# Gathers issued two at a time in the first graph layer and in the attention, and a node's own product moved to the end of the second graph layer

## The chip, the cores and the metric

The kernel runs on one core of one Trainium2 chip. The metric is the device time in microseconds. The engines are called as the profile calls them: PE (TensorE), PEld (its weight loads), DVE (VectorE), ACT (ScalarE), POOL (GpSimd) and SP (SyncE, which here only issues DMAs).

## What is computed

Four layers work on 6250 nodes of 256 values in fp32, each on the layer norm of the nodes, each added to them:

```
x += gnn0(norm(x))    # h = relu([x[src], edge_attr] @ W1 + b1) over 106250 edges sorted by dst;
                      # mean of h over each node's edges; relu([x, mean] @ W2 + b2)
x += moe0(norm(x))    # graph attention over 131072 random edges and own loops gives 16 values
                      # a node, a gate of the top 2 of 4 experts; the experts are 256-512-256, gelu
x += gnn1(norm(x))    # below
x += moe1(norm(x))    # shared network and top 2 of 4 small experts
```

The third one is where a product moves:

```
h   = relu(x @ Wp.T + bp)                       # 128 values a node
agg = segment_sum(edge_vals * h[src]**2, dst)
return h @ W1.T + b1 + sqrt(agg) @ W2.T + b2
```

`h @ W1.T` is the node's own product. It depends on no edge.

## The kernel before

Nodes lie in 49 tiles of 128 (T = 49). `x_all` and `b_all` keep 49 x 256 values a partition in SBUF for the whole kernel: `x_all` the running sum, `b_all` what the present layer needs of each node. The program is fully unrolled. The tile framework puts in the semaphores and may move an instruction on its engine's queue ahead of others that wait; otherwise the order is that of the code. Three tables lie in DRAM and are gathered from: `y_dram` (x @ W1 for the first layer, 256 values a node), `gat_dram` (24 values) and `hp_dram` (128 values). A `gather` (L1103) is one indirect DMA on POOL's queue: 128 rows, one to a partition. DMAs other than gathers go on SP's queue, a few on ACT's.

**Start** (L1310 to L1359): the nodes are loaded and normed, `y_dram` is written, edge windows are made.

**Stage 1, first graph layer** (L1362 to L1546). For each tile of 128 nodes a window of 18 x 128 edges is taken in three groups of six (`groups1`, G1 = 6). A group's edge values come on SP (`load_attr`), its six source rows by six gathers into one tile `yg` of [P, 6, D], three of them in turn (`load_sources`, L1382). Work goes by pairs of 128 edges (`pairs`, NPC = 3 a group): `turn` transposes a pair on PE, with ACT copying it out; `hidden` multiplies (four products of 256 columns), adds the gathered rows on DVE (L1417) and takes the Relu on ACT into `hbuf` (L1422); once a group `add_up` sums over nodes with 0/1 matrices (L1443). The loop L1523 runs `turn` three pairs ahead and `hidden` one pair ahead. At the second pair of a group (L1534) `load_sources` is called for two groups on; its tile is free when the group before is through `hidden`. For the groups 1 to 3 a copy of one column of `hbuf` into `seen` on POOL (L1386) holds the gathers until a named activation is done. `end_of` finishes a tile of nodes in pieces between the pairs. A generator, `background`, sorts the attention's edges on DVE.

**Stage 2, attention and experts** (L1554 to L2153). The attention's sorted edges come in 80 groups of 8 x 128 (NA = 80, G = 8). The loop L2113 does one group a turn, in a pipeline five deep: `fetch(k)` at the head of the turn issues eight gathers into the tile `sg` (five in turn), `score` works on group k - 2, `weigh` on k - 3, `spread_out` on k - 4 and `add_up` on k - 5. `weigh` and the first half of `spread_out` (L1743) read the gathered rows; the latter frees the tile. Between these stand six calls of `slot`, written out by hand. A `slot` advances the experts by one piece (`experts1`: `first` makes products and gelu, L1607, into `hh`, two in turn; `second` the second product, with its sums stored to DRAM) and every waiting step of `node_values` by one.

`node_values` (L1949) ends the layer for two tiles of nodes and begins the next one: it adds the experts' outputs with their gates to `x_all` (L1956), norms (L1976), adds the row b1 + b2 of the second graph layer to `x_all` (L1980), transposes (L1987), copies out to `b_all` (L1988), multiplies by Wp (L1992), takes the Relu into a small tile `ht` (L1994), transposes that into one half of a PSUM tile `py` (L1998), multiplies `ht` by `w1t` into the other half (L1999), squares the first half (L2001), adds the second half to `x_all` (L2002) and stores the square to `hp_dram` (L2003). The pool of `py` has two buffers, which the experts' second product uses too.

**Stage 3, second graph layer's edges and the last network** (L2160 to L2469). 139 groups of six chunks of 128 edges: `fetch` gathers four groups ahead (six buffers, L2382), `weights_of` makes weighted 0/1 matrices on DVE (L2390), `add_up` sums on PE (L2411). When a block of nodes has all its edges, `roots` takes the square root (L2423) and `end_of2` multiplies by W2 (`w2t`, L2228), adds to `x_all` (L2229), norms, transposes into `b_all` and makes the gate's logits. Then `gates2` and `experts2` work on the block, in pieces between the groups. There are 10 blocks of four tiles, three of two and three of one.

Of the kernel before, what the change touches and what calls it, by code (L numbers as in the profile page):

```python
# [8 lines left out]
F32 = mybir.dt.float32  # L9
# [832 lines left out]
def kernel(ctx: ExitStack, tc: tile.TileContext, a: dict, out: bass.AP):  # L842
# [74 lines left out]
    with ExitStack() as fast:  # L917
# [362 lines left out]
        with ExitStack() as layer:  # L1280
# [81 lines left out]
            with (  # L1362
# [8 lines left out]
                hbuf = [wy.tile([P, G1, WS], F32, name=f"h{i}") for i in range(2)]  # L1371
                seen = wy.tile([P, 1], F32, name="seen")
                sources, equals, et, sums = {}, {}, {}, {}
# [7 lines left out]

                def load_sources(q):  # L1382

                    if 1 <= q <= 3:
                        p, j = (q - 2, G1 - 1) if q > 1 else (0, 0)
                        GP.tensor_copy(seen, hbuf[p % 2][:, j, 0:1])  # L1386
                    w, g = groups1[q]
                    sources[q] = wk.tile([P, G1, D], F32, name="yg", bufs=3)
                    for j, (k, t) in enumerate(chunk(g)):
                        gather(sources[q][:, j, :], y_dram, src1[:, w, k, t : t + 1])  # L1390

# [15 lines left out]
                def hidden(k):  # L1407
                    q, j = pairs[k]
                    ph = psh.tile([P, 2, D], F32, name="ph")
                    e = et.pop(k)  # L1410
                    for i in range(2):
                        mm(
                            ph[:, i, :], lambda c: e[:, i, c * P : (c + 1) * P],
                            lambda c: w1b[:, c, :],
                        )
                    y = sources[q][:, j : j + 2, :]
# [5 lines left out]
                    SC.activation(h[:, j : j + 2, 0:D], y, AF.Relu)  # L1422
# [94 lines left out]
                work = [background()]  # L1517
                load_sources(0)
                for k in range(3):
                    turn(k)  # L1520
                hidden(0)
                load_sources(1)
                for k in range(len(pairs)):  # L1523
                    if k + 3 < len(pairs):
                        turn(k + 3)
                    if k + 1 < len(pairs):
                        hidden(k + 1)

                    q = k // NPC
                    if k % NPC == 0 and q:  # L1530
                        add_up(q - 1)
                    if k == len(pairs) - 1:
                        add_up(q)
                    if k % NPC == 1 and q + 2 < len(groups1):  # L1534
                        load_sources(q + 2)
                    for n in list(work):
                        if next(n, work) is work:
                            work.remove(n)
                    if k % (NPC * NG) == 0 and k:
                        work.append(end_of(k // (NPC * NG) - 1))  # L1540
                    if k == len(pairs) - 1:
                        work.append(end_of(T - 1))
# [28 lines left out]
        def experts1():  # L1571
# [24 lines left out]
            def first(u, f0):  # L1596
# [9 lines left out]
                for f in (f0, f0 + 1):  # L1606
                    SC.activation(  # L1607
                        hidden[u][:, f, :n, :], ph[:, f - f0, :n, :], AF.Gelu,
                        bias=b1[:, e, f : f + 1],
                    )  # L1610

            def second(u, i):
# [37 lines left out]
        def advance(queue, n):  # L1650
            for _ in range(n):
                if queue and next(queue[0], queue) is queue:
                    queue.pop(0)

        layers = [experts1()]
        part = sums.tile([P, 3, T, H], BF16, name="part")
        with (
# [32 lines left out]

            def fetch(g):
                got[g] = wk.tile([P, G, GW], F32, name="sg", bufs=5)
                for j in range(G):
                    gather(got[g][:, j, :], gat_dram, src2[:, g * G + j : g * G + j + 1])
# [234 lines left out]
            with nc.allow_non_contiguous_dma(reason="a bias, one element a partition"):  # L1929
                SY.dma_start(bp, a["L1_gnn_bp"].rearrange("(c p) -> p c", p=P))  # L1930
            w1t = w6.tile([P, D], F32, name="w1t")
            SY.dma_start(w1t, a["L1_gnn_W1_T"])
            b1 = bcast_row(w6, "b1", a["L1_gnn_b1"])
            V.tensor_add(b1, b1, bcast_row(n6, "xn", a["L1_gnn_b2"]))
            ys = {}
# [13 lines left out]
            def node_values(ws):  # L1949
# [22 lines left out]
                )  # L1972
                xns, hts = {}, {}
                for i, w in enumerate(ws):
# [4 lines left out]
                    )  # L1979
                    V.tensor_add(x_all[:, w, :], x_all[:, w, :], b1)  # L1980
                    yield False
# [8 lines left out]
                for w in ws:  # L1990
                    ph = psy.tile([P, 2, D], F32, name="py")[:, 0, 0:P]
                    mm(ph, lambda c: wpt[:, c, :], lambda c: b_all[:, w, c * P : (c + 1) * P])  # L1992
                    hts[w] = n6.tile([P, P], F32, name="ht")
                    SC.activation(hts[w], ph, AF.Relu, bias=bp)  # L1994
                    yield False
                for w in ws:
                    py = psy.tile([P, 2, D], F32, name="py")
                    TE.transpose(py[:, 0, 0:P], hts[w], ident)  # L1998
                    mm(py[:, 1, :], lambda c: hts[w], lambda c: w1t, 1)  # L1999
                    hp = n6.tile([P, PD], F32, name="hp")  # L2000
                    SC.activation(hp, py[:, 0, 0:P], AF.Square)  # L2001
                    V.tensor_add(x_all[:, w, :], x_all[:, w, :], py[:, 1, :])  # L2002
                    SY.dma_start(nodes(hp_dram)[:, w, :], hp)  # L2003
                    yield False
# [108 lines left out]
            for k in range(NA + 5):  # L2113
                if k < NA:
                    fetch(k)
                if k == 1:
                    own_edges()
                now, here, there, before = k - 2, k - 3, k - 4, k - 5
                if 0 <= before < NA:
                    add_up(before, 0)  # L2120
                slot()
                if now in range(NA):
                    score(now, 0)
                slot()
                if here in range(NA):
                    weigh(here)
# [3 lines left out]
                run(routing, False)  # L2130
                slot()
                if 0 <= before < NA:
                    add_up(before, 1)
                slot()
                if now in range(NA):
                    score(now, 1)
# [27 lines left out]
        with (  # L2164
# [8 lines left out]
            w2t = wp.tile([P, D], F32, name="w2t")  # L2173
            SY.dma_start(w2t, a["L1_gnn_W2_T"])
            gw = load_rows(wp, "gw", a["L1_ffn_gW"])
            gb = bcast_row(wp, "gb", a["L1_ffn_gb"])
# [46 lines left out]
            def end_of2(b, i, root):  # L2223
# [3 lines left out]
                pm = psm.tile([P, D], F32, name="pt")  # L2227
                mm(pm, lambda c: root[:, i, :], lambda c: w2t, 1)  # L2228
                V.tensor_add(x_all[:, w, :], x_all[:, w, :], pm)  # L2229
# [189 lines left out]
            def roots(b):  # L2419
                n = blocks[b][1]  # L2420
                root = wk.tile([P, BT, P], F32, name="gt")[:, 0:n, :]
                pe = sums.pop(b)[:, 0 : n * P].rearrange("p (w k) -> p w k", k=P)
# [118 lines left out]
```

## Time and profile before

| | |
|---|---|
| median of the runs, us | 3580.82 (3578.01 to 3580.89, three runs) |
| the profiled execution's own time, us | 4368.05 |
| its span, first to last instruction, us | 4366.3 |
| mean granted PE clock in it | 0.866 |
| instructions | 57680 |
| gathers in stages 1, 2, 3 | 882, 640, 831 |
| first and last gather start, us | 131.5 and 1674.3; 1713.7 and 2984.1; 3074.0 and 4286.1 |
| moved by DMA, mean | 428.52 MB, 98 GB/s |

The profile is of one execution, whose own time is longer than that of the runs without a profile. In a line of a group the columns are: code line, engine, operation, tile written <- tiles read, count; then the busy time in us and the mean of one in ns; then how long the engine had been idle before such instructions, with what ended most of that idle time. "issue" is idle time in which the engine waited for nothing that the profile shows; "remote" is a release that it cannot place. A product of fp32 operands stands in the trace as two records, each with its weight load.

### The profile page before, as it was taken

To read this page: it belongs to the slowest core of one execution; us is meant where nothing else is said; L and a number is where in the kernel's file an instruction comes from. 1 tells how busy PE (TensorE), PEld (TensorE's weight loads), DVE (VectorE), ACT (ScalarE), POOL (GpSimd) and SP (SyncE) were. 2 spreads that over 40 slices of the span, in tenths; PEclk is the share of its full clock that TensorE was granted. 3 is DMA by queue.
4 is the path that set the end of the run, shared out by engine and by line. 5 is a ranking of instruction groups with operands and counts; after the bars stand their busy time and mean duration, and the time that the engine had idled before them with its cause. 6 is when DMAs were issued, how large, how long until landed. Compare 5 with 4: busy or idle time off the path is not lost.

```text
span 4366.3 us, 57680 instructions
## 1 busy us (share of the span) xinstructions
PE 3529.8 (81%) x20063; PEld 2739.8 (63%) x20063; DVE 2183.1 (50%) x6292; ACT 1397.3 (32%) x2752; POOL 2243.2 (51%) x2367
## 2 busy tenths in 40 slices
PE   8788899998989987787888889888435776767888
PEld 3566666666666766576777777677334554544666
DVE  9788774333433333565646464656222343333445
ACT  4333333333333333232443433445001111211223
POOL 0455555555555554445444444442566666666651
PEclk9899999999999999899999999989557676776778
DMA  5445545555445443222424232333211121111210
GB/s 155 125 149 157 138 155 160 153 150 157 146 147 160 146 145 99 68 72 63 110 69 112 63 107 67 93 85 89 61 47 46 51 57 50 50 51 49 55 47 25
DMA packets 342929, 428.52 MB, mean 98 GB/s; under 512 B 139174, under 2 KB 246453, under 8 KB 342630
## 3 DMA queue, kind: packets, MB, share of 16 engines
q1 hardware_dynamic: 245174, 244.98, 18.7%
q0 software_dynamic: 89408, 178.08, 16.1%
q8 instruction: 162, 2.65, 0.2%
q10 hardware_dynamic: 8048, 1.68, 0.2%
q14 instruction: 137, 1.12, 0.1%
HBM read 382.05 MB, written 42.49 MB: 97 GB/s over the span
## 4 chain that ended last, share of the span: by engine, by line
PE 61%; another core or an unknown queue 11%; issue 11%; DVE 10%; ACT 4%; DMA 1%; POOL 1%; SPq 0%; DVEq 0%; ACTq 0%
PE ph L1091 26%; PE py L1091 10%; PE pt L1085 7%; PE pe L2411 5%; PE pe L1443 5%; PE po L1771 3%; PE pt L1091 3%; DVE key L1240 1%; PE pa L1708 1%; DMA rb<-low_dram 1%; DVE order L1237 1%; DVE eq L2390 1%; DVE pp L1750 1%; ACT L1607 1%
## 5 line engine op out<-in xcount | busy, mean ns | idle before, releaser
L1104 POOL DMA_INDIRECT yg<-y_dram,src x882 | 841.7, 954 | 822.8 <-ACT h L1422 338.7
L1104 POOL DMA_INDIRECT hg<-hp_dram,src x831 | 784.4, 944 | 446.3 <-issue 227.5
L1104 POOL DMA_INDIRECT sg<-gat_dram,src x640 | 611.6, 956 | 663.7 <-DVE px L1743 333.3
L1091 PE MATMUL ph<-w1b,et 128*128 128x256 f32 x3528 | 887.9, 394 | 28.0 <-issue 25.3
L1091 PEld LDWEIGHTS ph<-w1b,et 128*128 128x128 f32 x3528 | 662.9, 198 | 122.7 <-issue 45.6
L1417 DVE TENSOR_TENSOR yg<-ph,yg 128x512 f32<-128x512 f32 x441 | 299.8, 686 | 496.4 <-PE ph L1091 172.9
L2411 PEld LDWEIGHTS pe<-eq,hg 128*128 128x128 f32 x2036 | 377.7, 264 | 210.7 <-issue 143.5
L2411 PE MATMUL pe<-eq,hg 128*128 128x96 f32 (+15 forms) x2036 | 386.9, 344 | 146.4 <-issue 87.0
L1091 PE MATMUL py<-w,hh 128*128 128x256 f32 x1568 | 414.0, 402 | 61.3 <-ACT hh L1607 40.3
L2390 DVE TENSOR_SCALAR eq<-px,dst,ew 128x96 f32<-128x96 f32 x831 | 261.0, 367 | 320.4 <-remote 129.9
L1091 PE MATMUL ph<-b_all,w 128*128 128x256 f32 (+1 forms) x1600 | 410.7, 397 | 4.8 <-issue 4.7
L1086 ACT ACTIVATE et<-pt 128x512 f32<-128x512 f32 x441 | 259.5, 594 | 411.5 <-PE pt L1085 222.1
L1091 PEld LDWEIGHTS py<-w,hh 128*128 128x128 f32 x1568 | 298.7, 199 | 115.3 <-ACT hh L1607 47.8
L1422 ACT ACTIVATE h<-yg 128x512 f32<-128x512 f32 x441 | 275.6, 629 | 229.3 <-DVE yg L1417 180.7
L1091 PEld LDWEIGHTS ph<-b_all,w 128*128 128x128 f32 x1600 | 306.9, 201 | 45.7 <-issue 8.1
L1085 PE MATMUL pt<-ident,ea 128*128 128x128 f32 x1764 | 288.8, 285 | 33.6 <-issue 18.0
L1443 PE MATMUL pe<-h,eq 128*32 128x257 f32 x3168 | 254.1, 387 | 62.6 <-issue 35.2
L1085 PEld LDWEIGHTS pt<-ident,ea 128*128 128x128 f32 x1764 | 218.1, 148 | 110.5 <-issue 69.9
L1771 PE MATMUL po<-pp,B 128*128 128x240 f32 (+10 forms) x1280 | 269.2, 350 | 21.8 <-issue 12.1
L1607 ACT ACTIVATE hh<-ph,b 128x256 f32<-128x256 f32 (+1 forms) x400 | 165.7, 467 | 367.2 <-remote 130.4
L1771 PEld LDWEIGHTS po<-pp,B 128*128 128x128 f32 x1280 | 227.0, 198 | 38.9 <-issue 13.9
L1443 PEld LDWEIGHTS pe<-h,eq 128*32 128x32 f32 x3168 | 104.5, 109 | 190.4 <-issue 92.7
(331 smaller groups left out, 4328.3 us busy)
## 6 DMA issues: line engine op xcount, KB each, us to landing
ea<-in_edge_attr_dram SPq DMA_DIRECT2D x147, 768.0 KB
y<-y SPq DMA_DIRECT2D x196, 128.0 KB
w<-in_L_ffn_W_dram SPq DMA_DIRECT2D x48, 512.0 KB
y<-ys SPq DMA_DIRECT2D x96, 256.0 KB
rb<-low_dram SPq DMA_DIRECT2D x80, 256.0 KB
yg<-y_dram,src POOLq DMA_INDIRECT x882
hg<-hp_dram,src POOLq DMA_INDIRECT x831
sg<-gat_dram,src POOLq DMA_INDIRECT x640
```

The lines of the kernel that those rows point to most:

```text
L1085: TE.transpose(pt[:, c, :], src[:, c * P : (c + 1) * P], ident)
L1086: SC.activation(dst, pt.rearrange("p c k -> p (c k)"), AF.Copy)
L1091: TE.matmul(dst, lhs(c), rhs(c), start=c == 0, stop=c == n - 1)
L1104: GP.indirect_dma_start(out=dst, out_offset=None, in_=table[0:NP, :], in_offset=IndirectOffsetOnAxis(ap=idx, axis=0),)
L1237: V.max(out=top, in_=key)
L1417: V.tensor_add(y, ph, y)
L1422: SC.activation(h[:, j : j + 2, 0:D], y, AF.Relu)
L1443: TE.matmul(sums[w][b * Q : (b + 1) * Q, :], eq[k][:, j, at], h[:, i * NT + j, :], start=g == 0 and j == NT - 1, stop=g == last_of[b] and ...
L1607: SC.activation(hidden[u][:, f, :n, :], ph[:, f - f0, :n, :], AF.Gelu, bias=b1[:, e, f : f + 1],)
L1771: TE.matmul(po.rearrange("p b v -> p (b v)"), B[:, j, :], pp[:, j, 0:n, :].rearrange("p b v -> p (b v)"), start=half == 0 and j == 0, stop ...
L2390: V.tensor_scalar(equals[k][:, j, :], lanes[:, 0:NW], dst_of[:, t : t + 1], ew[:, t : t + 1], op0=OP.is_equal, op1=OP.mult,)
L2411: TE.matmul(sums[b][:, lo - t0 * P : hi - t0 * P], hg[:, j, :], eq[:, j, lo - n0 : hi - n0], start=False, stop=after >= (t0 + n) * P,)
```

## The change

In the **first layer**, `load_sources` takes a pair rather than a group. Its tile is [P, 2, D], nine in turn, so the memory is the same. For the pairs 3 to 8 a copy on POOL writes the first column of the new tile from an activation in `hbuf`, and the gathers follow into the same tile. The loop calls it up to twice a pair until it is six pairs ahead, then once a pair. A tile is free when the pair three before the present one is through `hidden`.

In the **attention**, `fetch` takes two chunks rather than eight, and is called four times a turn, after the first, second, third and fourth `slot`. From the second group on, a copy on POOL ahead of each two gathers writes one column of their rows from the newest expert activation (`newest`, set at the end of `first`).

In the **second graph layer**, the Relu's result is written over the first half of the tile's row in `b_all`, where it stays. The product by `w1t`, its add to `x_all` and the add of the bias row leave `node_values`. In stage 3 `end_of2` makes both products into one PSUM tile, `roots` adds the bias row to a whole block, and `w1t` and the two bias rows are loaded at the stage's head.

```diff
-                def load_sources(q):
-
-                    if 1 <= q <= 3:
-                        p, j = (q - 2, G1 - 1) if q > 1 else (0, 0)
-                        GP.tensor_copy(seen, hbuf[p % 2][:, j, 0:1])
+                def load_sources(k, after):
+
+                    q, j = pairs[k]
                     w, g = groups1[q]
-                    sources[q] = wk.tile([P, G1, D], F32, name="yg", bufs=3)
-                    for j, (k, t) in enumerate(chunk(g)):
-                        gather(sources[q][:, j, :], y_dram, src1[:, w, k, t : t + 1])
+                    sources[k] = wk.tile([P, 2, D], F32, name="yg", bufs=3 * NPC)
+
+                    if NPC <= k < 3 * NPC:
+                        p, i = pairs[after]
+                        h = hbuf[p % 2][:, i, 0:1]
+                        GP.tensor_copy(sources[k][:, :, 0:1], h.unsqueeze(1).to_broadcast([P, 2, 1]))
+                    for i, (n, t) in enumerate(list(chunk(g))[j : j + 2]):
+                        gather(sources[k][:, i, :], y_dram, src1[:, w, n, t : t + 1])
...
                     if k + 1 < len(pairs):
                         hidden(k + 1)
+                    for _ in range(2):
+                        if loaded < min(k + 2 * NPC + 1, len(pairs)):
+                            load_sources(loaded, k + 1)
+                            loaded += 1
...
-                    if k % NPC == 1 and q + 2 < len(groups1):
-                        load_sources(q + 2)
...
+                newest[0] = hidden[u][:, f0, 0, 0:1]
...
-            def fetch(g):
-                got[g] = wk.tile([P, G, GW], F32, name="sg", bufs=5)
-                for j in range(G):
+            def fetch(g, j0):
+
+                if j0 == 0:
+                    got[g] = wk.tile([P, G, GW], F32, name="sg", bufs=5)
+                if g > 0:
+                    GP.tensor_copy(
+                        got[g][:, j0 : j0 + 2, 0:1],
+                        newest[0].unsqueeze(1).to_broadcast([P, 2, 1]),
+                    )
+                for j in range(j0, j0 + 2):
                     gather(got[g][:, j, :], gat_dram, src2[:, g * G + j : g * G + j + 1])
...
-                    V.tensor_add(x_all[:, w, :], x_all[:, w, :], b1)
...
-                    hts[w] = n6.tile([P, P], F32, name="ht")
-                    SC.activation(hts[w], ph, AF.Relu, bias=bp)
+
+                    SC.activation(b_all[:, w, 0:P], ph, AF.Relu, bias=bp)
...
-                    TE.transpose(py[:, 0, 0:P], hts[w], ident)
-                    mm(py[:, 1, :], lambda c: hts[w], lambda c: w1t, 1)
+                    TE.transpose(py[:, 0, 0:P], b_all[:, w, 0:P], ident)
                     hp = n6.tile([P, PD], F32, name="hp")
                     SC.activation(hp, py[:, 0, 0:P], AF.Square)
-                    V.tensor_add(x_all[:, w, :], x_all[:, w, :], py[:, 1, :])
...
                 slot()
+                if k < NA:
+                    fetch(k, 0)
                 if now in range(NA):
                     score(now, 0)
                 slot()
+                if k < NA:
+                    fetch(k, 2)
...
                 slot()
+                if k < NA:
+                    fetch(k, 4)
...
                 slot()
+                if k < NA:
+                    fetch(k, 6)
...
-                mm(pm, lambda c: root[:, i, :], lambda c: w2t, 1)
+                mm(
+                    pm, lambda c: (b_all[:, w, 0:P], root[:, i, :])[c],
+                    lambda c: (w1t, w2t)[c],
+                )
...
             def roots(b):
                 n = blocks[b][1]
+                at = slice(blocks[b][0], blocks[b][0] + n)
+                V.tensor_add(
+                    x_all[:, at, :], x_all[:, at, :],
+                    b12[:, None, :].to_broadcast([P, n, D]),
+                )
```

More of the change, by code (lines that the diff above doesn't have):

```diff
@@ L1371 @@
                 hbuf = [wy.tile([P, G1, WS], F32, name=f"h{i}") for i in range(2)]
-                seen = wy.tile([P, 1], F32, name="seen")
                 sources, equals, et, sums = {}, {}, {}, {}
@@ L1415, in hidden @@
                         )
-                    y = sources[q][:, j : j + 2, :]
+                    y = sources.pop(k)
                     V.tensor_add(y, ph, y)
@@ L1517 @@
                 work = [background()]
-                load_sources(0)
+                for k in range(NPC):
+                    load_sources(k, None)
                 for k in range(3):
@@ L1521 @@
                 hidden(0)
-                load_sources(1)
+                loaded = NPC
                 for k in range(len(pairs)):
@@ L1653, in advance @@
                     queue.pop(0)
+        newest = [None]
         layers = [experts1()]
@@ L1930 @@
                 SY.dma_start(bp, a["L1_gnn_bp"].rearrange("(c p) -> p c", p=P))
[L1931 to L1934, printed above, removed]
             ys = {}
@@ L1972, in node_values @@
                 )
-                xns, hts = {}, {}
+                xns = {}
                 for i, w in enumerate(ws):
@@ L2113 @@
             for k in range(NA + 5):
-                if k < NA:
-                    fetch(k)
                 if k == 1:
@@ L2174 @@
             SY.dma_start(w2t, a["L1_gnn_W2_T"])
+            w1t = wp.tile([P, D], F32, name="w1t")
+            SY.dma_start(w1t, a["L1_gnn_W1_T"])
+            b12 = bcast_row(wp, "b12", a["L1_gnn_b1"])
+            V.tensor_add(b12, b12, bcast_row(wp, "b2", a["L1_gnn_b2"]))
             gw = load_rows(wp, "gw", a["L1_ffn_gW"])
```

## The prediction, made before the result was known

> **What bounds the kernel now.** I read the page's busy lines and slices first, then busy time by stage, then the waits of the lines that the change touches, and last the start times of single instructions. The page (engine, busy us, share of the span; below them the span in 40 slices, in tenths):
>
> ```profile
> PE 3529.8 (81%) x20063; PEld 2739.8 (63%) x20063; DVE 2183.1 (50%) x6292; ACT 1397.3 (32%) x2752; POOL 2243.2 (51%) x2367
> ...
> PE   8788899998989987787888889888435776767888
> ...
> POOL 0455555555555554445444444442566666666651
> PEclk9899999999999999899999999989557676776778
> ```
>
> The PE row changes at slice 28, and POOL is fuller after it. Busy time by stage (start, the first graph layer, attention with the experts, the second graph layer with the last network; columns are length, then busy us of each engine, granted clock, DMA share, GB/s):
>
> ```profile
> 0.00:130.00 130.00, 106.15 (x306) 51.18 (x306) 123.63 (x379) 61.88 (x160) 0.71 (x7) 0.97 0.47 140
> 130.00:1700.00 1570.00, 1399.98 (x9092) 1060.95 (x9093) 800.67 (x2124) 571.31 (x1225) 842.29 (x885) 0.95 0.51 149
> 1700.00:3074.00 1374.00, 1140.72 (x7141) 967.28 (x7140) 789.96 (x2013) 539.83 (x952) 615.77 (x644) 0.93 0.33 83
> 3074.00:4366.00 1292.00, 882.92 (x3526) 660.39 (x3526) 468.85 (x1779) 224.29 (x416) 784.42 (x831) 0.69 0.18 48
> ```
>
> In stages 1 and 2 TensorE is busy 89% and 83% at nearly full clock: they are TensorE's. In stage 3 it has 68% at a low clock. There the gathers set the pace. POOL's groups (busy, mean ns of one, idle before them), then two of its waits in stage 3 (us, times, longest):
>
> ```profile
> L1104 POOL DMA_INDIRECT yg<-y_dram,src x882 | 841.7, 954 | 822.8 <-ACT h L1422 338.7
> L1104 POOL DMA_INDIRECT hg<-hp_dram,src x831 | 784.4, 944 | 446.3 <-issue 227.5
> L1104 POOL DMA_INDIRECT sg<-gat_dram,src x640 | 611.6, 956 | 663.7 <-DVE px L1743 333.3
> ```
>
> ```profile
> POOL hg L1104 <- remote: 107.6, 35, 6.0
> ...
> POOL hg L1104 <- PE pe L2411: 65.4, 18, 7.9
> ```
>
> One gather is 0.945 us and 0.30 us of issue follow: 1.25 us from start to start. 831 of them are 1039 us of the 1212 between the first start (3074) and the last (4286); POOL waits 107.6 + 65.4 = 173 us, 14%, mostly for buffers that TensorE has not finished with.
>
> **The profiled execution and the median.** The profiled one took 4368 us (span 4366), the median is 3581: 787 us less. Floors from spacing say where these are not. A 256-column fp32 record is 0.216 us after the one before it in unbroken runs, a 128-column one 0.109. Stage 1: 3528 x 0.216 + 1764 x 0.109 + 3168 x 0.054 (four quarters side by side) + some 85 for the ends of nodes = 1210 us. Stage 2: 3168 x 0.216 = 684, po 217, pa and counting 56, node values 58 = 1015. Stage 3: POOL's 1039, and the 80 after the last gather. With the start's 130: 3474, an estimate. So unprofiled all stalls together are some 107 us, where the profiled execution has 892. Terms that are work at pace I carry over whole, terms that are stalls at about a third.
>
> **What the Trainium skill says.** "TensorE: Matmul & The Clock Gate", What's actually happening: the array's clock is halved until it has been busy. The trace agrees: the w2t records of stage 3 stand 0.426 us apart at the median against 0.218 for the w1t ones of stage 2. "Perfetto Trace Analysis", DMA Instruction — SWDGE (GPSIMD): the end shown is that of making descriptors, not of the data. The trace agrees: at the start of stage 3 the data land 2.40 us after the issue on the chain. "SBUF — State Buffer", Who interferes with whom: some VectorE instructions lock GpSimd out. Here it hardly shows: yg gathers have minimum 940, median 946 and maximum 2060 ns.
>
> **The change, part by part.**
>
> *Node's own product out of stage 2.* The groups, then three lines of who waited for L2002 (us, times):
>
> ```profile
> L1091 PE MATMUL py<-w1t,ht 128*128 128x256 f32 x98 | 30.7, 397 | 0.0
> L1980 DVE TENSOR_TENSOR x_all<-x_all,b 128x256 f32<-128x256 f32 x49 | 20.3, 418 | 7.7 <-ACT xn L1976 6.9 <-ACT b_all L1988 0.5
> L2002 DVE TENSOR_TENSOR x_all<-x_all,py 128x256 f32<-128x256 f32 x49 | 20.2, 414 | 16.5 <-ACT hp L2001 12.2 <-issue 4.2
> ```
>
> ```profile
>   PE py L1998: 21.5, 9
>   PEld py L1987: 20.7, 8
>   PE py L1987: 17.6, 7
> ```
>
> (a) TensorE loses 98 x 0.218 = 21 us of pace, in a stage that is its own: -21, whole. (b) The PSUM buffer py is freed by the square (L2001), not by VectorE's add (L2002). That is 0.45 to 5.7 us sooner, 1.38 on average over the 49 pairs in the trace. The PE matmul waits are 21.5 + 17.6 = 39 us (the weight loads' waits are the same time again); part would wait for the square or for something else: I take half, -20 profiled, -7 at the median; ends 0 and -39. (c) VectorE loses 40.5 us. It is busy 790 of 1374, so I count none; if it paced the stage, up to -40. (d) The Relu goes into b_all rather than ht: same instruction, 0. (e) In the tail of stage 2 (3030 to 3074) the last nodes are a chain of single instructions, with some four adds and two products off it: -3.
>
> *The same product in stage 3.* (f) 98 records more in end_of2; w2t, the nearest row, has 45.3 us busy for its 98 in this stage, 21 at full clock. The new product reads b_all and w1t, loaded long before, and stands next to w2t, so no wait is added. (g) VectorE: ten adds of 128x1024 at 1.22 us (nearest: 1.215 for L1783), three of 512 at 0.69, three of 256 at 0.42: 15.5 us, of 1292 with 469 busy. Behind them in VectorE's queue stand the equality tiles (L2390) that add_up needs. Both lie beside POOL's gathers while TensorE keeps within the six gather buffers. It fails to in 14% of the time, so 14% of 45.3 + 15.5 = 8.6 reaches POOL; I take +8 profiled, +6 at the median. Cover gone: +45 and more. (h) After the last gather some six nodes are still to end: +3. (i) Three loads move from SP's queue in stage 2 to the head of stage 3, at about 0.4 us each, where the last hp stores still pass: 0 to +1.2, taken as 0, as VectorE waits 2.9 us there for those stores anyway.
>
> *Gathers in twos, attention.* The same 640 gathers, plus 79 x 4 = 316 copies on POOL, each waiting for the newest expert activation. Nearest: the three `seen` copies, 183 to 197 ns; from copy to gather 0.35 us from start to start. 316 x 0.35 = 111 us more for POOL, which has 616 + 166 of issue in 1374: covered. Behind each copy only gathers are queued; weigh needs them three turns later, some 45 us. ScalarE writes the hh buffer anew two units on, some eight slots, so it should not wait for a copy: 0, bounds 0 to +10.
>
> *Gathers in twos, first layer.* As many gathers, three copies more (1 us on POOL, free). Pair 3's gathers now wait for pair 1's activation, not pair 0's: up to 3 us later while POOL fills the pipeline: +2. Steadily, POOL needs 2 x 1.25 = 2.5 us a pair against TensorE's 1210 / 441 = 2.7; waits for gather data are only 13.1 us in the whole tile's list.
>
> *Runs of gathers.* Adding up every start-to-start distance on TensorE beyond 0.45 us: in the first four gathers of an unbroken POOL run it lost 11 of 670 us (stage 1) and 23 of 376 (stage 2); from the fifth gather on 57 of 441 and 60 of 431. The run of 40 gathers at 1713 to 1764 has TensorE at one bf16 record in 1.4 to 2.1 us. Twos break such runs. But the cause may be the recording itself, since in the median all stalls are 107 us: I take -15 profiled, -5 at the median; ends 0 and -117.
>
> Sum, profiled: -21 - 20 - 3 + 8 + 3 + 2 - 15 = -46, 4368 to 4322. At the median: -21 - 7 - 3 + 6 + 3 + 2 - 5 = -25: **3556 us**.
>
> **Rivals.** *The runs are real* (0.18): half of the 107 us of stalls goes with them. Then -55 for -5: 3506. For it: the counts above. Against: stage 3 has the longest runs and no such budget. *Stage 3 takes it back* (0.16, slower): TensorE's add_up, not POOL, paces it wherever buffers are returned late. All 45.3 us of (f) then reach the end, with the 3 of (h): -34 + 48 = +14, 3595. It decides once TensorE's work for a group of six exceeds POOL's 7.5 us; for it, POOL's 173 us of waits and the 16.8% that add_up's products have on the chain from 3400 to 4200; against, the 25.9% that an unknown queue (the gathers' data) has there. *The change doesn't do what it says* (0.13): stage 2 is paced by the chain from scores through VectorE and ScalarE, and the freed TensorE time becomes a wait for DVE za or ACT hh (TensorE's second expert product waits 40.3 us for ACT hh as it is). Then (a) and (b) give -9 for -28 and the runs 0: 3581 - 9 - 3 + 11 = 3580.
>
> **How the numbers follow.** The forecast has 0.53, with 3537 to 3567 as its own range: (b) and (c) at their full ends, a third of 20 and of 40, make -19 or so more, the copies and (i) at theirs +11. The range runs from the first rival's time, with half of its cases beyond it, to just past the slower one: 3505 to 3600. About 0.2%, 7 us, is what a measurement can tell from no change. Faster by more: 0.53 + 0.18 = 0.71; within: 0.13; slower: 0.16.
>
> **What would show it.** Right: in stage 2 no L2002 in TensorE's waits, PE busy down by about 31, the stage 25 to 60 us shorter; in stage 3 the w-products at 196 records, POOL's gather spacing still 1.25 us, its waits up by under 15 us. Wrong: stage 3 longer by over 30 us; ScalarE's gelu waiting for a POOL copy; weigh waiting for gather data; or stages 2 as long as before with TensorE idler.

## The result, and the profile after

The changed kernel takes **3559.13 us** (median of five runs, 3557.47 to 3560.89), the kernel before, run beside it, 3578.01 (3574.05 to 3580.89). The ratio is 0.9947 (95% interval 0.9935 to 0.9958): 19 us or 0.5% less. The forecast was 3556.

One thing has to be known to read any number here: on three other chips these kernels take some 700 to 800 us longer, with 4368 to 4384 us for the kernel before (the **long level**, as against the **short level** of 3578 to 3581); the profiled execution of before that the prediction read is of the long level, while the medians that it forecast and the profile after are of the short one. So below, each kernel is compared with the kernel before on its own chip, and stages only between profiles of one level.

The page of the changed kernel, the same rows as shown of before (engine, busy us, share of the span; then 40 slices in tenths):

```profile
PE 3324.9 (93%) x20063; PEld 2646.0 (74%) x20063; DVE 2170.9 (61%) x6210; ACT 1412.2 (40%) x2750; POOL 2308.9 (65%) x2686
...
PE   7999999999999999999999999997678888889898
...
POOL 0376666666666664777666666773777777777773
PEclk9999999999999999999999999998566777777797
```

TensorE's row is 9 from the second slice to the last whole one of the attention. In before's page it went between 7 and 9 there. Its busy time is 205 us *less* than before's for the same 20063 records: that is the level, not the change. By stage (the bounds are the first gathers of this profile; columns as before: length, busy us of PE, PEld, DVE, ACT, POOL, granted clock, DMA share, GB/s):

```profile
131.00:1430.00 1299.00, 1293.75 (x9156) 1028.89 (x9157) 810.25 (x2154) 596.46 (x1241) 841.04 (x889) 1.00 0.60 181
1430.00:2471.00 1041.00, 1014.53 (x6981) 895.40 (x6979) 759.75 (x1891) 527.80 (x933) 680.44 (x959) 0.99 0.42 109
```

```profile
2471.00:3510.00 1039.00, 875.13 (x3416) 643.13 (x3416) 449.04 (x1662) 202.63 (x361) 785.78 (x830) 0.73 0.20 59
```

In stage 1 TensorE is busy 1294 of 1299 us, in stage 2 1015 of 1041. In stage 3 POOL's 831 gathers take 1039 us from the first start to the last, 1.25 us each: an unbroken row. The groups of the gathers, which answer to those of before (busy, mean ns | idle before them):

```profile
L1104 POOL DMA_INDIRECT yg<-y_dram,src x882 | 840.0, 952 | 542.3 <-ACT h L1424 183.8 <-issue 181.0 <-ACT et L1086 141.6
...
L1104 POOL DMA_INDIRECT hg<-hp_dram,src x831 | 786.7, 947 | 268.1 <-issue 223.7 <-DMA hg<-hp_dram,src 24.7 <-DMA eb<-in_L_ffn_eb_dram 15.1
...
L1104 POOL DMA_INDIRECT sg<-gat_dram,src x640 | 620.1, 969 | 195.0 <-issue 134.5 <-POOL sg L1703 45.7 <-DMA wpt<-in_L_gnn_Wp_T_dram 3.8
```

The gathers of stage 3 had 446 us of idle time before them and 173 of it on TensorE and unplaced releases. Now 224 of the 268 are issue. Who waited for the attention's tiles (us, times) shows the new copies (L1703) doing what the prediction listed as a sign against it, three times:

```profile
  POOL sg L1104: 46.9, 172
  ACT hh L1612: 9.7, 3
  DVE z L1745: 1.4, 1
```

What stage 2 gained can't be read against before's profile, as the levels differ. The experiments give profiles of the short level with stages 1, 2 and 3 as in the kernel before.

### The profile page after: what moved, and what is told of

Read it like the earlier page. It is cut to its first block, busy times and chain, and to the rows that moved or that the text cites. A ratio compares the mean times of both kernels' runs of the same rounds, so it can differ in the third digit from the quotient of the medians.

```text
span 3557.3 us, 58534 instructions
## 1 busy us (share of the span) xinstructions
PE 3324.9 (93%) x20063; PEld 2646.0 (74%) x20063; DVE 2170.9 (61%) x6210; ACT 1412.2 (40%) x2750; POOL 2308.9 (65%) x2686
## 4 chain that ended last, share of the span: by engine, by line
PE 65%; POOL 14%; issue 7%; DMA 7%; DVE 6%; ACT 1%; SPq 1%; ACTq 0%; POOLq 0%; DVEq 0%
PE ph L1091 31%; POOL hg L1104 12%; PE py L1091 10%; PE pt L1085 6%; PE pe L1445 5%; PE po L1785 5%; DMA hg<-hp_dram,src 5%; PE pt L1091 2%; PE pe L2431 2%; PE pa L1722 1%; POOL sg L1104 1%; DMA rb<-low_dram 1%; DVE junk L982 1%; DVE order L1237 1%; DVE key L1240 1%
## 5 line engine op out<-in xcount | busy, mean ns | idle before, releaser
L1091 PE MATMUL ph<-w1b,et 128*128 128x256 f32 x3528 | 835.8, 380 | 0.0
L1091 PEld LDWEIGHTS ph<-w1b,et 128*128 128x128 f32 x3528 | 637.1, 190 | 68.7
L2431 PE MATMUL pe<-eq,hg 128*128 128x96 f32 (+15 forms) x2036 | 436.2, 349 | 164.9 <-DMA hg<-hp_dram,src 135.6
L1091 PE MATMUL py<-w,hh 128*128 128x256 f32 x1568 | 384.4, 385 | 4.9 <-ACT hh L1612 4.5
L1091 PE MATMUL ph<-b_all,w 128*128 128x256 f32 (+1 forms) x1600 | 386.4, 380 | 1.7 <-ACT hh L1612 1.7
L1091 PEld LDWEIGHTS ph<-b_all,w 128*128 128x128 f32 x1600 | 289.7, 190 | 33.9 <-ACT hh L1612 2.3
L1085 PE MATMUL pt<-ident,ea 128*128 128x128 f32 x1764 | 272.2, 277 | 4.0 <-ACT et L1086 4.0
L1785 PE MATMUL po<-pp,B 128*128 128x240 f32 (+10 forms) x1280 | 252.3, 337 | 2.4 <-DVE acc L1791 2.2
L1785 PEld LDWEIGHTS po<-pp,B 128*128 128x128 f32 x1280 | 215.5, 190 | 14.7 <-DVE acc L1791 3.3
L1445 PE MATMUL pe<-h,eq 128*32 128x257 f32 x3168 | 218.1, 386 | 3.2 <-ACT h L1424 2.1
```

Source lines behind the costliest of these rows:

```text
L1085: TE.transpose(pt[:, c, :], src[:, c * P : (c + 1) * P], ident)
L1091: TE.matmul(dst, lhs(c), rhs(c), start=c == 0, stop=c == n - 1)
L1445: TE.matmul(sums[w][b * Q : (b + 1) * Q, :], eq[k][:, j, at], h[:, i * NT + j, :], start=g == 0 and j == NT - 1, stop=g == last_of[b] and ...
L1785: TE.matmul(po.rearrange("p b v -> p (b v)"), B[:, j, :], pp[:, j, 0:n, :].rearrange("p b v -> p (b v)"), start=half == 0 and j == 0, stop ...
L2431: TE.matmul(sums[b][:, lo - t0 * P : hi - t0 * P], hg[:, j, :], eq[:, j, lo - n0 : hi - n0], start=False, stop=after >= (t0 + n) * P,)
```

## The experiments

"The twos" are the gathers issued two at a time; a "row" is several gathers issued without a pause, so groups of six and eight make longer rows than twos. Two theories stand against each other. **Mine:** the gain is TensorE's 98 records that leave stage 2, and the twos do next to nothing. **The rival:** the twos break rows of gathers that hold TensorE up, and the move is a small matter. Stage lengths below are from first gather to first gather; "tail" is from the last gather's start to the end.

### The parts alone, at the short level

**c_product**, the move alone: the change without the parts in `load_sources`, `fetch` and the two loops. Its core:

```diff
-                    mm(py[:, 1, :], lambda c: hts[w], lambda c: w1t, 1)
-                    V.tensor_add(x_all[:, w, :], x_all[:, w, :], py[:, 1, :])
...
+                mm(
+                    pm, lambda c: (b_all[:, w, 0:P], root[:, i, :])[c],
+                    lambda c: (w1t, w2t)[c],
+                )
```

> The product moved to the second graph layer's end, the gathers left as before. My theory: this is nearly the whole gain, -21 (TensorE's pace in stage 2) -7 (PSUM tile freed by the square) -3 (stage 2's tail) +6 (stage 3) +3 (after the last gather) = -22 us against the kernel before, 3556 to 3558. Rival 'the runs of gathers are real': -10 or less, since most of the 19 us came from the twos. Rival 'stage 3 takes it back': 0 to +14. Its profiled execution: if the 787 us between the profile and the median belong to the runs of eight and six gathers, it is again near 4350; if they belong to that one profile, it is near 3560.

Measured: 3556.25 us (3554.19 to 3560.64) against 3580.98, ratio 0.9935 (0.9921 to 0.9948): -23 us. The whole gain is here; the rival's "-10 or less" is out. Its profile keeps the rows of eight and six gathers and has a span of 3558.9 us, so such rows alone do not bring the 787 us.

**ab_twos**, the twos alone: the other parts of the diff, without the move.

```diff
-            if k < NA:
-                fetch(k)
...
+            if k < NA:
+                fetch(k, 0)
```

> Gathers in twos in the first layer and in the attention, the product left in stage 2. My theory: +2 for the first layer's start, -5 for the broken runs: -3 us, within 0.2% of the kernel before. Rival 'the runs are real': -12 to -50. A third possibility, that the 316 copies on POOL or the later gathers cost something: +5 to +20, and then the move alone gains more than 19.

Measured: 3582.00 against 3580.98, ratio 1.0008 (1.0000 to 1.0016): nothing, or up to 6 us lost.

**a_twos**, twos in the first layer alone (`load_sources` and its loop).

```diff
+                    for _ in range(2):
+                        if loaded < min(k + 2 * NPC + 1, len(pairs)):
+                            load_sources(loaded, k + 1)
+                            loaded += 1
```

> Twos in the first layer alone. My theory: +2 at the start of stage 1, -2 for the runs: 0 us, within 0.2%. 'The runs are real': -6 to -25. Stage 1 in its profile: if the runs of six cause the profile's stalls, stage 1 is near 1280 us as in the changed kernel and stage 2 near 1374 as in the kernel before; if it is something of the one profile, all stages are short or all long.

Measured: 3584.27 against 3580.98, ratio 1.0007 (0.9999 to 1.0015). All stages of its profile are short, those with long rows of gathers too, so the 787 us go with the execution and not with such rows alone.

**b_twos**, twos in the attention alone (`fetch`, `newest` and their calls).

```diff
+                if g > 0:
+                    GP.tensor_copy(
+                        got[g][:, j0 : j0 + 2, 0:1],
+                        newest[0].unsqueeze(1).to_broadcast([P, 2, 1]),
+                    )
```

> Twos in the attention alone. My theory: 316 copies on POOL at 0.35 us are covered, the runs give -3: -3 us, within 0.2%. 'The runs are real': -6 to -25. If ScalarE's gelu waits for the copies (three waits, 9.7 us in the profile of the changed kernel): +5 to +10.

Measured: 3579.78 against 3580.98, ratio 1.0001 (0.9992 to 1.0009). The 316 copies are hidden; the three waits of ScalarE for a copy (9.7 us in the changed kernel) reach nothing.

The stages of these four and of the changed kernel, us:

| kernel | stage 1 | stage 2 | gathers of stage 3 | tail |
|---|---|---|---|---|
| a_twos (stages 2 and 3 as before) | 1298.6 | 1064.3 | 1036.0 | 48.5 |
| b_twos (stages 1 and 3 as before) | 1296.5 | 1063.6 | 1037.2 | 47.9 |
| ab_twos | 1299.6 | 1060.7 | 1036.1 | 48.5 |
| c_product | 1297.1 | 1040.7 | 1038.9 | 48.8 |
| changed kernel | 1298.8 | 1041.1 | 1038.7 | 47.3 |

The move takes 20 to 24 us from stage 2 and gives back 2 to 3 in stage 3, nothing in the tail. The busy times of stage 2, first of a_twos (product still in it), then of c_product, columns as above:

```profile
1431.00:2494.00 1063.00, 1035.92 (x7075) 912.33 (x7073) 779.95 (x1981) 530.80 (x935) 615.91 (x643) 0.99 0.43 107
2494.00:3530.00 1036.00, 870.12 (x3321) 633.24 (x3322) 442.11 (x1652) 201.54 (x357) 782.67 (x830) 0.71 0.22 59
```

```profile
1430.00:2471.00 1041.00, 1013.52 (x6981) 895.91 (x6979) 758.67 (x1892) 528.02 (x933) 617.78 (x643) 0.99 0.44 109
2471.00:3510.00 1039.00, 887.13 (x3410) 652.64 (x3411) 448.55 (x1660) 200.95 (x356) 786.02 (x830) 0.71 0.22 59
```

PE has 94 records fewer in the window and 22.4 us less to do (1035.92 - 1013.52), and the stage is 22 us shorter; TensorE's idle time in it is 27 us in both. What leaves TensorE leaves the stage. In stage 3 the same records are 17 us more of PE's time (887.13 - 870.12), and 3 us of it show. TensorE's waits in stage 2 of a_twos (us, times, longest), where L2007 is the add that was L2002, say what the held PSUM tile cost there:

```profile
PE py L1091 <- ACT hh L1612: 6.3, 5, 2.5
...
PE py L2003 <- DVE x_all L2007: 0.2, 1, 0.2
```

0.2 us, where before's profile had 39. That the 22 us are TensorE's time, and not VectorE's adds, is read from these rows and not shown by an experiment; the kernels made to isolate it fell on chips of the long level, as follows.

One thing the diff does not show: nine of the sixteen bias adds in `roots`, 10.9 us of VectorE, run in the last 10.5 us of stage 2, among the last nodes' norms, and not beside the gathers of stage 3. In c_product (L2422 is the bias add, L1963 to L1966 the norm of the last tile of nodes):

```profile
2460.02 0.19 ACT L1963 ACTIVATE ln_rs<-ln_rs 128x1 f32<-128x1 f32 x1
...
2460.62 1.22 DVE L2422 TENSOR_TENSOR x_all<-x_all,b 128x1024 f32<-128x1024 f32 x1
...
2461.76 0.15 DVE L1965 RECIPROCAL ln_rs<-ln_rs 128x1 f32<-128x1 f32 x1
...
2462.96 0.15 DVE L1966 SCALAR_TENSOR_TENSOR off<-ln_mv,ln_rs 128x1 f32<-128x1 f32 x1
```

That tile's normed values (`xn`) are begun 3.6 us after its L1963 ends here (2460.21 to 2463.81), and 0.55 us after it in a_twos. That some 3 us of gain lie there is an estimate from these two figures; no kernel without this order was run.

### One half of the move at a time, at the long level

**no_product**: of stage 2 only TensorE's product goes; VectorE's add stays and reads the other half of the PSUM tile.

```diff
-                    mm(py[:, 1, :], lambda c: hts[w], lambda c: w1t, 1)
...
-                    V.tensor_add(x_all[:, w, :], x_all[:, w, :], py[:, 1, :])
+                    V.tensor_add(
+                        x_all[:, w, :].rearrange("p (c k) -> p c k", k=P),
+                        x_all[:, w, :].rearrange("p (c k) -> p c k", k=P),
+                        py[:, 0:1, 0:P].to_broadcast([P, 2, P]),
+                    )
```

> The kernel before, with only the product by w1t left out of stage 2; its add to the running sum stays, of the same size, and reads the transposed half of the PSUM tile in the product's place (so the second graph layer's own product is missing from the output). VectorE's work and its hold on the PSUM tile are as before, only TensorE's 98 records go. If stage 2 is TensorE's (step a): -21 us. If it was VectorE's adds or the held PSUM tile: 0 to -5. The moved product gave -23 in all, with +3 of it in stage 3.

Measured: 4374.39 us, against 4384.50 for the kernel before on that chip: ratio 0.9989 (0.9971 to 1.0008). No effect to speak of.

**no_adds**: the product stays, both adds go.

```diff
-                    V.tensor_add(x_all[:, w, :], x_all[:, w, :], b1)
...
-                    V.tensor_add(x_all[:, w, :], x_all[:, w, :], py[:, 1, :])
```

> The kernel before with the product by w1t kept in stage 2, but neither it nor the row b1 + b2 added to the running sum (both are missing from the output). VectorE loses 98 adds, 40 us, and the PSUM tile is freed by the square; TensorE's work is as before. My steps b and c: -7 us. If VectorE or the held tile were the cause of the whole gain: -20 or more. If neither matters when unprofiled: within 0.1% of the kernel before.

Measured: 4365.29, ratio 0.9963 (0.9946 to 0.9980): -16 us (9 to 24). So at this level the halves have changed places: TensorE's product is worth nothing that shows, and the held tile or VectorE's adds, which this kernel doesn't tell apart, cost something.

**no_product_2** is no_product once more.

> The same kernel as no_product (only TensorE's product by w1t left out of stage 2 and of the output). Where the kernel before takes about 3580 us, stage 2 has TensorE busy 97 in 100, so step a gives -21 to -23 us; the adds and the held PSUM tile, for which TensorE waits 2 to 3 us there, would leave it at 0 to -5. Where the kernel before takes about 4384, -0.1% again.

Measured: 4383.06 against 4379.17, ratio 1.0001 (0.9983 to 1.0020); the long level again, and again nothing. The waits of TensorE in stage 2 of no_product_2 and of no_adds:

```profile
PE py L1998 <- DVE x_all L2001: 24.9, 8, 4.6
...
PE py L1987 <- DVE x_all L2001: 18.0, 9, 5.0
```

```profile
PE py L1986 <- ACT hp L2000: 11.3, 7, 3.5
PE py L1997 <- ACT hp L2000: 9.4, 6, 2.4
```

With the add in place TensorE waits 43 us for it (L2001 here), product or no product. Without the adds 21 us of waits for the square are left: about half, as step (b) had guessed for before's profile.

**before_again**, the kernel before, unchanged, for a second profile.

> The kernel before once more, unchanged, for a second profile of it. If the 787 us between its profile and its median belong to that one profile: a span near 3575 us, stage 1 near 1280, stage 2 near 1063, gathers of stage 3 in 1036 to 1040. If a profile of this kernel always shows them: a span near 4350 us.

Measured: 4399.62 us, one run, on the chip of the 4384.50. The rows of its page:

```profile
PE 3492.0 (79%) x20063; PEld 2732.0 (62%) x20063; DVE 2183.6 (50%) x6292; ACT 1394.5 (32%) x2752; POOL 2245.9 (51%) x2367
...
PE   7788888888888895888888888888336766767787
```

This is the profile that the prediction read, once more: TensorE at 79% (81% there), with a stage 3 of 6 and 7. The stages are 1563.8, 1389.4, 1235.0 and 78.7 us. Between these two profiles of one program the stages differ by up to 29 us, so at the long level I use single stage lengths only for larger differences.

### The twos at the long level

**four_products**: the changed kernel, with its own product made four times in stage 3.

```diff
-                    pm, lambda c: (b_all[:, w, 0:P], root[:, i, :])[c],
-                    lambda c: (w1t, w2t)[c],
+                    pm, lambda c: (*[b_all[:, w, 0:P]] * 4, root[:, i, :])[c],
+                    lambda c: (w1t, w1t, w1t, w1t, w2t)[c], 5,
```

> The changed kernel with its own product made four times over in stage 3 (the output has it four times). 294 records more at 0.22 to 0.46 us each: 64 to 135 us of TensorE's work beside the gathers. If POOL's gathers cover it as they did the first 98 (+3 us in stage 3): +8 us or so against the changed kernel, that is 3567 us. If my 14% holds: +9 to +19, 3568 to 3578. If TensorE paces stage 3 (rival 'stage 3 takes it back'): +64 to +135, 3623 or more.

It was meant to test POOL's cover in stage 3. It ran beside 4384.50: 4282.22 us, ratio 0.9777 (0.9747 to 0.9806). With *more* work than the changed kernel it is some 100 us faster than before; the two halves of the move above came to 0 and 16.

**ab_twos_2**, the twos alone once more.

> The same kernel as ab_twos. Where the kernel before takes about 4384 us: if TensorE's stalls there belong to long runs of gathers, the twos take away -80 to -140 us (rival 'the runs are real', on that chip); if not, within 0.3%, and the 102 us that the changed kernel with four products won there come from the move. Where the kernel before takes about 3580: 0 to +3 us, as in the first run.

Measured: 4276.82 against 4379.17, ratio 0.9760 (0.9733 to 0.9788): **-102 us at the median** (93 to 117 by the ratio) from the edit that gave nothing on the first chip. Here the rival is right. Its stages are 1530.7, 1303.5, 1226.1 and 78.2 us: against before_again -33 in stage 1, -86 in stage 2; against no_product_2, on the same chip and with no gain over before, -33 and -84.

Where it comes from is seen best at the head of stage 2, where POOL has 40 gathers to issue at once. Fifty microseconds from the first of them, of c_product (short level, eights), before_again (long level, eights) and ab_twos_2 (long level, twos):

```profile
1430.00:1480.00 50.00, 48.29 (x393) 40.89 (x391) 39.53 (x108) 23.48 (x41) 38.03 (x39) 1.00 0.45 115
```

```profile
1695.00:1745.00 50.00, 13.68 (x75) 10.40 (x74) 8.52 (x24) 3.61 (x5) 38.02 (x40) 0.60 0.22 47
```

```profile
1660.00:1710.00 50.00, 34.31 (x212) 27.57 (x211) 22.62 (x63) 14.33 (x25) 33.34 (x46) 0.80 0.36 92
```

Under the same unbroken row of gathers TensorE starts 393 matmul records in one profile and 75 in the other, and ScalarE 41 instructions and 5. POOL itself is the same, 38 us for 39 and 40 gathers. With pauses in the row TensorE gets to 212. Part of that stretch in before_again, TensorE alone, in order of time (start, length, in brackets the idle time before and what ended it):

```profile
1703.37 0.54 PE L1794 MATMUL py<-q,b 128*128 128x49 bf16 x8
1703.74 0.46 PE L2048 MATMUL py<-ident,ht 128*128 128x128 f32 x1
1712.16 5.41 PE L1091 MATMUL py<-w,hh 128*128 128x256 f32 x16 [7.97 <-issue]
```

TensorE stands still for 7.97 us and the profile has no wait for it ("issue"): no late buffer or data that it shows. A count over the whole of stages 1 and 2 agrees: of TensorE's start-to-start distances the part beyond 0.45 us, taken from the fifth gather of an unbroken row on, is 48 and 76 us in before_again, 35 and 32 in ab_twos_2, and in c_product 5 and 2. It moves by some us with the pause at which a row is taken to end. In all, inside such rows and outside, the two stages lose 412, 345 and 27 us by this count: the smaller part of what the long level costs lies in the rows.

Sorting TensorE's idle time by what ended it shows the twos' gain more directly. The two largest waits at "issue" in stage 2 of no_product_2 (eights), and the same two in ab_twos_2 (twos) on the same chip (us, times, longest):

```profile
PE py L1091 <- issue: 47.3, 22, 11.0
...
PE pa L1708 <- issue: 36.3, 29, 3.3
```

```profile
PE pa L1722 <- issue: 10.9, 18, 2.0
...
PE py L1091 <- issue: 7.1, 11, 1.9
```

Summed over stage 2, such idle time is 114 us in the first and 40 in the second: 74 us less, of a stage that is 84 shorter. In the seven profiles of the long level with eights it is 91 to 121, in the two with twos 40 each, and at the short level 0 to 3.

**a_twos_no_product**: a_twos with no_product's edit on top.

```diff
-                    mm(py[:, 1, :], lambda c: hts[w], lambda c: w1t, 1)
```

> The kernel with twos in the first layer alone, and in it only TensorE's product by w1t left out of stage 2 and of the output, its add kept. Where the kernel before takes about 3580 us, the twos gave +0.07% alone; so a step (a) of -21 to -23 us shows as 3557 to 3562, and adds or a held PSUM tile as the cause would leave it at 3577 or more. Where the kernel before takes about 4380, the product alone gave 0, so this is the first layer's share of the 103 us: -33 us by the length of stage 1 in the traces, and 0 to -10 if most of it was the attention's.

Measured: 4354.15 against 4367.84, ratio 0.9953 (0.9936 to 0.9969): -20 us by the ratio, -14 at the medians. Since the product alone gave nothing at this level, 14 to 20 of the 102 us are the first layer's. That the other 80 or so are the attention's follows by difference; no kernel with the attention's twos alone was run at this level, but the 74 us above are all in the attention's stage.

**c_four_products**: c_product with the same fourfold product as four_products.

> The move alone, with the own product made four times over in stage 3 (the output has it four times). Where the kernel before takes about 3580: POOL's gathers cover the 294 extra records as they did the first 98: 3556 + 8 = 3564 us; with my 14%: 3565 to 3575; TensorE pacing stage 3: 3620 or more. Where the kernel before takes about 4380: the move gives about 0 there and the extra records 10 to 25 us, so +0.2 to +0.6%; if the move were worth its 21 us there too, within 0.1%.

Measured: 4376.15 against 4367.84, ratio 1.0007 (0.9987 to 1.0028). Without the twos the move and 294 extra records come out even. That is the last case of the expectation, in which the move is worth its 21 us at this level too; the 16 us of no_adds point the same way, but the move was not run here without the extra records. Neither "TensorE paces stage 3" (392 records in all would have cost 180 us by the 45 us of w2t's row) nor free extra work fits at this level: the gathers of stage 3 took 1261.7 us, 27 to 50 more than in the two profiles of before, and the tail 83.9.

## Why the prediction was right, and where it was not

The sign, the size and the main step were right; the way from the profile to the median was not.

*(a) The product out of stage 2, -21.* Right: 22.4 us less of PE's busy time and a stage 20 to 24 us shorter at the short level. The reason given (TensorE is the stage's limit) holds better there than in the profile it came from: 97% busy for 83%. At the long level the step fails: no_product gave 0 twice, while TensorE's waits for the add stayed (39 us in before, 43 in no_product_2). That the stage is paced by such stalls and not by TensorE's work is read from these waits. "Carried over whole" was right for the median and wrong for the profiled sum.

*(b) The PSUM tile freed by the square, -20 profiled, -7 at the median.* The profiled half was about right where it belongs: no_adds gave -16, with (c) in it. At the median it is next to nothing: TensorE waits 0.2 us for that add. The step that failed is "terms that are stalls at about a third".

*(c), (d) at 0, (e) -3.* (c) and (d) are not contradicted: VectorE has 21 us less to do in the window of stage 2 and is busy 73% of it. It is 21 and not 40.5 because nine bias adds and a few smaller instructions took the place. (e) can't be told apart within the 20 to 24 us, of which (a) is 22; the term did not reckon with those nine adds.

*(f) and (g), +8 profiled, +6 at the median.* Right mechanism, too large: 17 us of TensorE's work and 6 of VectorE's were added beside the gathers, and 2 to 3 reached the end, as POOL's gathers run without a pause at the short level. VectorE's are 6 and not 15.5 because nine of the adds had run in stage 2. The 14% of uncovered time that the term rests on belongs to the long level. There, c_four_products shows cover giving way.

*(h) the tail, +3.* Nothing: 47.3 to 48.8 us with and without the product.

*The first layer's start, +2.* Stage 1 is 1298.6 us in a_twos and 1296.5 in b_twos, and the ratio 1.0007: of the size forecast, at the edge of what can be measured. The attention's copies, 0: right, 1.0001.

*Runs of gathers, -15 profiled, -5 at the median.* Too small at the long level, where the twos gave -102, within the stated ends of 0 and -117; nothing at the short one. The counts over the trace were sound. The sentence that failed is "the cause may be the recording itself": runs without a profile also take 4384 us on such a chip, so the stalls are real.

So the sum, term by term at the median: forecast -21 - 7 - 3 + 6 + 3 + 2 - 5 = -25; measured some -22 in stage 2, +2 to +3 in stage 3, 0 in the tail, +2 in the first layer, 0 for the runs: -17, with -19 (15 to 23) for the whole. Over-counted gains in (b) and the runs, 12 us, were half paid for by over-counted costs in (f) to (h), 6 to 7: that 3556 came within 3 us of 3559 is in part luck.

**Rival B** (3506, "the runs are real") is out for the median. Its cause is there at the long level, where the twos gave more than the 55 us it allowed. **Rival C** ("stage 3 takes it back") is out at the short level: gather spacing stayed 1.25 us. **Rival D** ("stage 2 is not TensorE's") is out for the median, and at the long level it describes what no_product did. Of the signs named: no wait of TensorE for L2002, 1.25 us, and waits of POOL up by under 15 us came true. PE's busy time fell by 22 us for 31 and the stage by 20 to 24 for 25 to 60, at a level where a record is shorter than in the profile read. ScalarE did wait for a POOL copy, and b_twos shows that it costs nothing.

**What stays open.** Why the same program has two levels. A row of gathers is where TensorE starves most plainly, but POOL's instructions take the same time at both levels (sg and hg at the median 0.945 us at the short level, 0.947 at the long one), so what TensorE is short of in that time is not seen. Slower DMA packets do not show as the cause: in the DMA queue of instructions a packet takes 1.00 us at the median in before_again and 0.98 in c_product, in SyncE's large queue 46 ns in both. Whether a level belongs to a chip or to a time was not tried: one chip was short, three others long. The changed kernel itself was run at the short level only; at the long one four_products stands for it. The move alone was not run at the long level, and the one product without its adds not at the short one. No version run here beats the changed kernel at both levels: c_product is no slower at the short level (0.9935 for 0.9947, intervals that overlap), but lacks the twos, which were worth 2.4% at the long one.

## What to carry to other kernels

When a profiled execution is much longer than the runs, find out first whether it is the same condition, before scaling stalls from one to the other: a stall that is a fifth of the time in one can be absent in the other, and then neither its whole nor a third of it is the estimate. Work moved from a stage whose limit is TensorE to one whose limit is the gathers' engine is worth its own length, here 22 us for 3. An edit that does nothing on one chip was worth 2.4% on another, so gathers that nobody needs yet are best not issued in one row. And look in the trace where a moved instruction ends up: nine adds written for one stage ran in the one before, among the instructions of its last chain.

## What the runs showed of the hardware that was not expected

The kernel before takes 3578 to 3581 us at the short level and, on other chips, 4368 to 4384 at the long one (22% more), with the same instructions and the same gather time. Beside an unbroken row of 40 gathers on POOL, TensorE starts 393 matmul records in 50 us at the short level and 75 at the long one. At the short level such rows do not disturb TensorE: in stage 2 of c_product, rows of 40 or more gathers fill 123 us, and TensorE loses 0.2 of them. The granted clock in stage 3 is 0.71 to 0.73 at the short level and 0.69 in before's profile, so the low clock there is not a mark of the long level. TensorE's busy share alone does not tell the clock: 84% goes with 0.71 to 0.73 in that stage, 83% with 0.93 in stage 2 of before. Nor do long pauses: beside the gathers of c_product's stage 3 the clock stood at half for 600 of 1039 us, and TensorE had two pauses over 2 us, of 2.0 and 5.5.
